# A decoder's output projection moved behind its attention, with query products among the heads

## The chip, the cores and the metric

One NeuronCore of a Trainium2 chip runs one program. The time is device microseconds of one execution. A core has TensorE (PE, matrix products, with PEld for its weight loads), VectorE (DVE), ScalarE (ACT) and GpSimd (POOL), each with an in-order queue of instructions; SP issues most transfers. TensorE writes to PSUM, in banks of 512 f32 columns by 128 partitions; everything else lives in SBUF, 128 partitions wide, or in device memory.

## What is computed

Two layers over `x`, 2 batches of 512 tokens by 1024, each a cross attention and a feed-forward part with a residual. The change is in the second layer's attention, all in f32 (abbreviated):

```python
x = x + _L1_xattn_ref(_layernorm(x), ctx_4096, ctx_4096, mask, wq, wk, wv, wo, 0)
x = x + _L1_ffn_ref(_layernorm(x), W_up, gate_w, expert_bias, lora_A, lora_B)

def _L1_xattn_ref(query, key, value, mask, wq, wk, wv, wo, curr_seq_pos):
    # 32 query heads, 8 key/value heads, 128 wide; 512 queries, 1024 keys
    q = rope(heads(query @ wq)); k = rope(repeat(heads(key @ wk))); v = repeat(heads(value @ wv))
    ...
```

then softmax of `q @ k.T / sqrt(128) + mask` over the keys, times `v`, the heads side by side (4096 wide), times `wo` (4096 x 1024).

## The kernel before

**Products in seven.** Every large product is cut in two by two blocks and computed with seven block products in place of eight (Strassen's scheme in Winograd's form): sums of the left blocks (`left_steps`), sums of the right blocks (`right_steps`), seven products, and sums of the results. `seven` (L258) makes a new result, `seven_onto` (L294) adds to rows that are there. `accumulate` (L343, the matmul is L345) issues one block product. An f32 matmul shows as two records in a trace.

**Queries.** `queries` (L664) makes the query heads, four at a time ("quads", eight of them); seven products of four 512-column matmuls give one head pair for both batches. Rope (L204 to L211) turns each result: two half copies on ACT, one product with the cosines on DVE (L207), a product with the sines and a sum (L210, L211) on DVE, or on POOL in the last quad. Seven quads run ahead of the attention, in a dense stretch; the last is spread over its first iterations.

**Attention.** `attention` (L851) is a software pipeline over 64 heads (batch 0's 32, then batch 1's). Iteration n issues three parts:
- scores of head n + 2 (L763, 8 matmuls of 512 columns); DVE adds the mask from PSUM (L777, four times);
- filler products on TensorE, and on DVE the maximum tree of head n + 2 over the keys (L785, L787, L789 of 1024 elements, L791 of 512; both inputs in SBUF), woven between the filler's own sums;
- transposes (L727) of head n's denominators, `turn_sum`, and later of head n + 2's maxima, `turn_maximum`, each followed by a reduction on DVE (L729) and a trip through device memory that spreads the row; the products with the values of head n (L826, 8 matmuls, in two halves); and for head n + 1 the exponential: DVE adds the negative maximum from PSUM (L809, 2048 elements, twice), ACT takes exp (L812, twice), POOL adds up the denominators (L815, L818, L819 of 1024 elements, L820 of 512).

POOL then normalises head n - 1 (L837). TensorE, DVE, ACT and POOL run in the written order here; transfers are ordered by the scheduler.

**The output projection** is the filler. A group of four heads (one key/value head) gives 512 of the 4096 columns; from iteration 5 on, `projection` (L839) adds a group's share to the rows of its batch: per 256 tokens by 1024, seven products of two 512-column matmuls, two of them for each row block. That is 14 block products a group, 3 or 4 (12 or 16 records) in each iteration, 28 matmuls a group and 448 in all. Its results are added on DVE (L312, L318) and on POOL (L300); the left sums of a group are four POOL instructions (L233 to L241). The sums of `wo` are made ahead, during the queries (`output_sums`, L692), and stored; `output_operand` (L709) loads them per group.

**Around it.** Rows of batch 0 are complete halfway through the attention, so its norm, statistics (L151, L152 in iterations 38 to 41) and transposes run among batch 1's heads, and its feed-forward part starts as the last heads end. SBUF is cut in slots: 14 of 8 KB, 17 of 4 KB, 10 of 2 KB per partition; PSUM in two double banks (`wide`, for scores and transposes) and four single ones (`b`).

## Time and profile before

| | us |
|---|---|
| median of 3 runs | 2437.01 (2436.92 to 2438.63) |
| profiled execution, span | 2432.8 |
| layer 1 and keys, values | 0 to about 640 |
| queries, dense | about 640 to 924 |
| attention: first to last score matmul | 924.5 to 2242.6 |
| last projections, feed-forward parts | to 2432.8 |

Between 1500 and 1600 us, well inside the attention, the engines were busy like this (stretch, its length, then busy time and instructions of PE, PEld, DVE, ACT and POOL, the granted clock, the DMA share and GB/s):

```profile
1500.00:1600.00 100.00, 100.00 (x259) 46.34 (x259) 86.65 (x78) 25.52 (x22) 73.26 (x37) 1.00 0.38 108
```

How to read what follows: a row of the timeline is start, length, engine, line, operation, result and inputs, partitions by elements, the number of merged instructions, and in brackets the idle time before it with what ended it. A matmul's end is modelled, and successive matmuls overlap by that tail, so the price of one is read from starts.

### The profile page before, as it was taken

To read this page: it belongs to the slowest core of one execution; us is meant where nothing else is said; L and a number is where in the kernel's file an instruction comes from. 1 tells how busy PE (TensorE), PEld (TensorE's weight loads), DVE (VectorE), ACT (ScalarE), POOL (GpSimd) and SP (SyncE) were. 2 spreads that over 40 slices of the span, in tenths; PEclk is the share of its full clock that TensorE was granted. 3 is DMA by queue.
4 is the path that set the end of the run, shared out by engine and by line. 5 is a ranking of instruction groups with operands and counts; after the bars stand their busy time and mean duration, and the time that the engine had idled before them with its cause. 6 is when DMAs were issued, how large, how long until landed. Compare 5 with 4: busy or idle time off the path is not lost.

```text
span 2432.8 us, 19529 instructions
## 1 busy us (share of the span) xinstructions
PE 2407.8 (99%) x6792; PEld 1195.1 (49%) x6792; DVE 1842.8 (76%) x1998; ACT 527.2 (22%) x623; POOL 1024.5 (42%) x543
## 2 busy tenths in 40 slices
PE   9999999999999999999999999999999999999999
PEld 4477458654444444444444444444444444444444
DVE  5849774345986556898888888888898988888753
ACT  1210221011222222322222222222223222222210
POOL 0000010210000002777676767667776767677531
PEclk9999999999999999999999999999999999999999
DMA  5437133013796221344223323442332243233501
GB/s 197 169 99 281 70 131 112 26 61 116 280 334 212 78 90 53 101 141 117 75 80 106 117 68 89 143 143 79 129 117 78 95 123 116 66 91 109 173 9 61
DMA packets 151506, 288.01 MB, mean 118 GB/s; under 512 B 32112, under 2 KB 49776, under 8 KB 149104
## 3 DMA queue, kind: packets, MB, share of 16 engines
q1 hardware_dynamic: 110880, 244.54, 30.6%
q10 hardware_dynamic: 40384, 41.70, 5.6%
q8 instruction: 54, 0.88, 0.1%
q0 software_dynamic: 144, 0.52, 0.1%
q14 instruction: 44, 0.36, 0.1%
HBM read 223.54 MB, written 63.18 MB: 118 GB/s over the span
## 4 chain that ended last, share of the span: by engine, by line
PE 55%; DVE 4%; issue 1%; POOL 0%; ACT 0%; POOLq 0%; DVEq 0%; ACTq 0%
PE b L345 20%; PE wide L763 16%; PE b L826 16%; PE wide L727 2%; DVE u L809 1%; DVE u L777 0%; DVE u L789 0%; DVE small L729 0%; DVE u L318 0%; DVE u L787 0%; PE b L967 0%; PE wide L192 0%; DVE u L791 0%; DVE u L785 0%; PE wide L1016 0%
## 5 line engine op out<-in xcount | busy, mean ns | idle before, releaser
L345 PE MATMUL b<-u,u 128*128 128x512 f32 (+1 forms) x3600 | 1384.5, 541 | 14.8 <-DVE u L283 4.2
L345 PEld LDWEIGHTS b<-u,u 128*128 128x128 f32 x3600 | 681.3, 191 | 684.0 <-issue 605.2
L826 PE MATMUL b<-u,u 128*128 128x512 f32 x1024 | 460.3, 592 | 0.0
L763 PE MATMUL wide<-u,u 128*128 128x512 f32 x1024 | 452.6, 593 | 2.6 <-DVE u L777 1.7
L815 POOL TENSOR_TENSOR u<-u 128x1024 f32<-128x1024 f32 x64 | 151.6, 2368 | 705.3 <-ACT u L812 696.8
L777 DVE TENSOR_TENSOR u<-wide,u 128x1024 f32<-128x1024 f32 x256 | 312.7, 1223 | 125.3 <-PE wide L763 125.1
L812 ACT ACTIVATE u<-u 128x2048 f32<-128x2048 f32 x128 | 244.7, 1911 | 665.1 <-DVE u L809 662.3
L763 PEld LDWEIGHTS wide<-u,u 128*128 128x128 f32 x1024 | 192.8, 190 | 250.9 <-issue 175.5
L809 DVE TENSOR_TENSOR u<-u,b 128x2048 f32<-128x2048 f32 x128 | 290.1, 2267 | 3.0 <-ACT b L805 3.0
L826 PEld LDWEIGHTS b<-u,u 128*128 128x128 f32 x1024 | 186.2, 192 | 184.6 <-issue 184.6
L300 POOL TENSOR_TENSOR u<-u,u 128x512 f32<-128x512 f32 x120 | 184.3, 1562 | 170.3 <-DVE u L312 134.6
L318 DVE TENSOR_TENSOR u<-u,b 128x512 f32<-128x512 f32 x200 | 135.6, 679 | 121.7 <-PE b L345 114.4
L818 POOL TENSOR_TENSOR u<-u,u 128x1024 f32<-128x1024 f32 x64 | 150.7, 2355 | 30.9 <-ACT u L812 30.7
L819 POOL TENSOR_TENSOR u<-u,u 128x1024 f32<-128x1024 f32 x64 | 150.8, 2356 | 5.0
L204 ACT ACTIVATE u<-u 64x512 f32<-64x512 f32 x72 | 45.2, 628 | 361.6 <-DVE u L283 162.5
L837 POOL TENSOR_TENSOR u<-u,u 128x512 f32<-128x512 f32 x64 | 115.0, 1797 | 18.4 <-DMA u<-row 18.4
L785 DVE TENSOR_TENSOR u<-u 128x1024 f32<-128x1024 f32 x64 | 113.0, 1765 | 0.0
L727 PEld LDWEIGHTS wide<-ident,u 128*128 128x128 f32 x512 | 79.9, 203 | 61.8 <-issue 55.7
L605 POOL TENSOR_TENSOR u<-u,u 128x1024 f32<-128x1024 f32 x8 | 20.2, 2528 | 213.0 <-DVE u L156 210.4
L787 DVE TENSOR_TENSOR u<-u,u 128x1024 f32<-128x1024 f32 x64 | 107.5, 1679 | 0.2
L820 POOL TENSOR_TENSOR u<-u 128x512 f32<-128x512 f32 x64 | 100.1, 1564 | 5.0
L1158 POOL DMA_DIRECT2D u<-in_b_dram x1 | 0.7, 717 | 229.1 <-PE b L345 229.1
(136 smaller groups left out, 1639.4 us busy)
## 6 DMA issues: line engine op xcount, KB each, us to landing
u<-row ACTq DMA_DIRECT2D x128, 256.0 KB, 3.5
u<-wo SPq DMA_DIRECT2D x64, 512.0 KB, 4.3
u<-in_wo_dram SPq DMA_DIRECT2D x48, 512.0 KB, 4.4
u<-in_wq_dram SPq DMA_DIRECT2D x32, 512.0 KB, 4.3
q<-u SPq DMA_DIRECT2D x64, 256.0 KB, 2.3
u<-in_wo_dram SPq DMA_DIRECT2D x16, 1024.0 KB, 8.0
wo<-u SPq DMA_DIRECT2D x32, 512.0 KB, 4.4
u<-q SPq DMA_DIRECT2D x64, 256.0 KB, 4.5
```

Source lines behind the costliest of these rows:

```text
L300: nc.gpsimd.tensor_tensor(c, c, what, ALU.add)
L318: nc.vector.tensor_tensor(c, c, acc, ALU.add)
L345: nc.tensor.matmul(acc, lhsT, rhs, start=start and k == 0, stop=k == len(pairs) - 1, skip_group_check=True,)
L727: nc.tensor.transpose(tr[:, t, :], src[:, t, :], ident)
L763: nc.tensor.matmul(sc[:, ts(n, HALF)], self.kT[:, ts(2 * j + n, P)], self.qT, start=True, stop=True,)
L777: nc.vector.tensor_tensor(self.e[j // 2][:, js, :], sc.rearrange("p (k q) -> p k q", k=2), mask[j], ALU.add)
L809: nc.vector.tensor_tensor(e, e, self.nmf.unsqueeze(1).to_broadcast([P, 4, S]), ALU.add)
L812: nc.scalar.activation(e, e, AF.Exp)
L815: nc.gpsimd.tensor_tensor(d, e[:, 0:2, :], e[:, 2:4, :], ALU.add)
L818: nc.gpsimd.tensor_tensor(d, d, e[:, 0:2, :], ALU.add)
L819: nc.gpsimd.tensor_tensor(d, d, e[:, 2:4, :], ALU.add)
L826: nc.tensor.matmul(self.acc, self.v[:, k, :], self.e[j][:, k % 4, :], start=(k == 0), stop=(k == NKT - 1),)
```

## The change

- The projection leaves the attention. Each head is normalised and stored, with the sums of the outer scheme made on POOL, as operands of seven products (`o_d[i]`, i = 1 to 7): `normalize` makes one difference of 256 elements, and for heads 16 to 31 three more sums with what `fetch_earlier` reloads of the head 16 before it.
- `two_level` computes each of the seven as seven again: 49 block products of 64, each 8 matmuls of 256 columns for either batch, 784 in all. Both batches share one weight operand. Its operand sums are DVE instructions (`tensor`), put off through `pending` in the attention.
- The first of the seven (`two_level(1, ...)`) starts in the attention, from iteration 56; the other six follow it, each with its loads made during the one before (`prefetch`).
- Query products become the filler. `query_unit` computes a unit (two heads for both batches) in seven steps of four 512-column matmuls; twelve units, 84 steps, go into iterations 2 to 55 by `count`; four begin before and end in iterations -2 to 1. Their weight sums are on DVE (four of 512 elements a unit: three at the first step, one at the second), their rope on DVE (L207's) and POOL (L210's and L211's). `chained` replaces `seven`, with fewer sums on DVE and more copies on ACT.
- The sums of `wo` (`output_sums`) move from DVE, ahead of the attention, to POOL in iterations 2 to 49: four of 512 elements in every three iterations.
- Heads alternate between the batches every four heads, so that a mask is fetched anew for each group of four (`fetch_mask`).
- The rows stay in device memory until the attention ends; the feed-forward part then takes token halves of both batches in place of batches.

```diff
...
+    def chained(product, emit):
+        at = {}
+        a = ps_b()
+        for i in (1, 2, 6, 5, 7, 3, 4):
+            if i in (2, 5):
+                c = ps_b()
+            acc = a if i in (1, 6, 7, 4) else c
+            product(i, acc, i in (1, 2, 5))
+            if i in (1, 6, 5):
+                at[i] = u2([P, HALF])
+                nc.scalar.copy(at[i], acc)
+            elif i == 4:
+                emit(1, 0, acc, True)
+            else:
+                held, place = {2: (1, (0, 0)), 7: (5, (1, 1)), 3: (6, (0, 1))}[i]
+                nc.vector.tensor_tensor(at[held], at[held], acc, ALU.add)
+                emit(*place, at[held])
...
+    def query_steps(q, m, eng, later):
+        def finish(i, j, src, in_psum):
+            dst = src
+            if in_psum:
+                dst = u2([P, HALF])
+                if later is not None:
+                    nc.scalar.copy(dst, src)
+                    src = dst
+            yield from rope_steps(dst, src, 0, ATT_SCALE, eng)
+            nc.sync.dma_start(q_d[j][4 * q + 2 * i + m], dst)
+        def emit(i, j, src, in_psum=False):
+            steps = finish(i, j, src, in_psum)
+            next(steps)
+            if later is None:
+                next(steps, None)
+            else:
+                later.append(steps)
+        return emit
...
+    def query_unit(q, m, h_ops, raw, s1, later, seven=chained):
+        w = dict(zip((1, 2, 7, 4), raw))
+        tensor = nc.vector.tensor_tensor
+        def product(i, acc, start):
+            accumulate(
+                acc, [(w[i][:, c, :], h_ops[i - 1][:, c, :]) for c in range(4)], start
+            )
+        for k, _ in enumerate(seven(product, query_steps(q, m, nc.gpsimd, later))):
+            if k == 0:
+                w[5] = s1()
+                tensor(w[5], w[7], w[4], ALU.add)
+                tensor(w[7], w[1], w[7], ALU.subtract)
+                w[6] = w[1]
+                tensor(w[6], w[5], w[1], ALU.subtract)
+            elif k == 1:
+                w[3] = w[2]
+                tensor(w[3], w[2], w[6], ALU.subtract)
+            yield k
...
+    def output_sums():
+        for c in range(NH // 2):
+            kq, c = divmod(c, 8)
+            t = u8([P, 2, 2, HALF])
+            for kh in range(2):
+                nc.sync.dma_start(
+                    t[:, kh], wo_v[:, 2 * kh + kq, c, :].rearrange("p (j n) -> p j n", j=2)
+            yield
+            b11, b12, b21, b22 = (t[:, kh, j] for kh in range(2) for j in range(2))
+            nc.gpsimd.tensor_tensor(b11, b12, b11, ALU.subtract)
+            nc.gpsimd.tensor_tensor(b12, b22, b12, ALU.subtract)
+            yield
+            nc.gpsimd.tensor_tensor(b22, b22, b11, ALU.subtract)
+            nc.gpsimd.tensor_tensor(b21, b21, b22, ALU.subtract)
+            for i, src in ((5, b11), (7, b12), (6, b22), (4, b21)):
+                nc.sync.dma_start(
+                    wo_t[i][:, kq, :, c, :], src.rearrange("p (q n) -> p q n", q=2)
+                )
+            yield
...
+            if self.n % GRP == GRP - 1 and self.n < B * NH - 1:
+                fetch_mask(1 - self.b, j)
...
+        def place(self, i):
+            return o_d[i][:, self.hd // 8 % 2, :, self.hd % 8, self.b, :]
+        def fetch_earlier(self):
+            self.earlier = u2([P, 2, 2, P])
+            for h, i in enumerate((0, 7)):
+                nc.sync.dma_start(self.earlier[:, h], self.place(i))
+            oT = self.oT
+            nc.gpsimd.tensor_tensor(oT, oT, self.den, ALU.mult)
+            halves = [oT[:, ts(h, QTR)].rearrange("p (t n) -> p t n", t=2) for h in range(2)]
+            more = u2([P, 2, 2, P])
+            diff = more[:, 0]
+            nc.gpsimd.tensor_tensor(diff, halves[1], halves[0], ALU.subtract)
+            if self.hd < NH // 2:
+                kept = {1: halves[0], 0: halves[1], 7: diff}
+            else:
+                hi, d = (self.earlier[:, h] for h in range(2))
+                nc.gpsimd.tensor_tensor(more[:, 1], d, halves[1], ALU.add)
+                nc.gpsimd.tensor_tensor(diff, d, diff, ALU.add)
+                nc.gpsimd.tensor_tensor(hi, hi, halves[1], ALU.add)
+                kept = {2: halves[0], 4: halves[1], 6: more[:, 1], 3: diff, 5: hi}
+            for i, t in kept.items():
+                nc.sync.dma_start(self.place(i), t)
+    total = B * NH
+    heads, kv, later, pending = {}, {}, [], []
...
+    def attention(fill, count, other, last):
+        for n in range(-2, total + 1):
+            fetch_values(n + 1)
+            if old and old.hd >= NH // 2:
+                old.fetch_earlier()
-            if n == GRP - 1 or n == NH:
-                fetch_rows(n // NH)
-            if GRP <= n <= total and n % GRP == 0:
-                oT = outs.pop(n // GRP - 1)
-                sums = u8([P, 3, 2, 256])
-                places = iter(range(3))
-                o_ops = left_sums(
-                    nc.gpsimd,
-                    oT[:, 0:2, 0:256],
-                    oT[:, 2:4, 0:256],
-                    oT[:, 0:2, 256:S],
-                    oT[:, 2:4, 256:S],
-                    lambda: sums[:, next(places)],
-                )
-                following = n // GRP - 1, o_ops
+            other(n)
-            k = (n - 1) % GRP
-            if n > GRP and k == 0:
-                gg, o_ops = following
-                stretches = projection(gg // NKV, o_ops, dict(w_ops))
-            for _ in range(3 + k % 2 if n > GRP else 0):
-                next(stretches, None)
-                next(tree, None)
-            if n > GRP and gg + 1 < B * NKV:
-                for i in {2: (1, 6, 2), 3: (7, 5, 4, 3)}.get(k, ()):
-                    w_ops[i] = output_operand((gg + 1) % NKV, i)
-            for i in range(extra.pop(n, 0)):
+            for i in range(count(n)):
-                next(extra["products"])
+                next(fill, None)
-            if n == GRP:
-                w_ops = {i: output_operand(0, i) for i in (1, 6, 2, 7, 5, 4, 3)}
-            if old:
+            if old and new:
+                if not new:
+                    old.turn_sum()
...
+            last(n)
+            yield
+    a_set, w_set = {}, {}
...
+    def first_sums(i):
+        a, w = a_set[i], w_set[i]
+        w["t1"] = [u4([P, 4, QTR]) for _ in range(2)]
+        for h in range(2):
+            yield tensor(w["t1"][h], w[0, 1][h], w[0, 0][h], ALU.subtract)
+            yield tensor(w[0, 1][h], w[1, 1][h], w[0, 1][h], ALU.subtract)
+        s1 = a["s1"] = u8([P, 8, B, P])
+        yield tensor(s1, a[0, 1], a[1, 1], ALU.add)
+        yield tensor(a[0, 1], a[0, 0], a[0, 1], ALU.subtract)
+    def two_level(i, block, fresh, op, put):
+        a, w = a_set[i], w_set[i]
+        banks = [ps_b(), ps_b()]
+        for k, (a_k, w_k, start, (x, y), first) in {
+            1: ((0, 0), (0, 0), True, (0, 0), True),
+            5: ("s1", "t1", True, (1, 1), True),
+            6: ((0, 0), (0, 0), False, (0, 1), True),
+            3: ("s1", (1, 1), False, (0, 1), False),
+            7: ((0, 1), (0, 1), False, (1, 1), False),
+            2: ((1, 0), (1, 0), True, (0, 0), False),
+            4: ((1, 1), "t1", False, (1, 0), True),
+        }.items():
+            acc = banks[k in (5, 3, 2)]
+            for b in range(B):
+                for c in range(8):
+                    nc.tensor.matmul(
+                        acc[:, ts(b, QTR)],
+                        a[a_k][:, c, b, :],
+                        w[w_k][c // 4][:, c % 4, :],
+                        start=start and b == 0 and c == 0,
+                        stop=c == 7,
+                        skip_group_check=True,
+                    )
+                if b == 0:
+                    yield
+            dst, src = block(x, y), acc.rearrange("p (b n) -> p b n", b=B)
+            if fresh and first:
+                nc.scalar.copy(dst, src)
+            else:
+                nc.vector.tensor_tensor(dst, dst, src, op)
+            if k == 1:
+                put(tensor(a[0, 0], a["s1"], a[0, 0], ALU.subtract))
+                for h in range(2):
+                    put(tensor(w[0, 0][h], w[1, 1][h], w["t1"][h], ALU.subtract))
+            elif k == 5:
+                put(tensor(a["s1"], a[1, 0], a[0, 0], ALU.subtract))
+            elif k == 7:
+                for h in range(2):
+                    put(tensor(w["t1"][h], w[1, 0][h], w[0, 0][h], ALU.subtract))
+            yield
...
+    def fill():
+        yield from chain(*early[:3])
+        raw = load_unit(2, 0)
+        yield from early[3]
+        for k in range(4, NH // 2):
+            for i in query_unit(*divmod(k, 2), h_ops, raw, lambda: u2([P, 4, P]), later):
+                if i == 4 and k + 1 < NH // 2:
+                    following = load_unit(*divmod(k + 1, 2))
+                yield
+            raw = following
+        r[0] = u8([P, 2, B, HALF])
+        yield from two_level(1, in_r, True, ALU.add, pending.append)
+    def count(n):
+        if n < 2:
+            return {-2: 6, -1: 6, 0: 4, 1: 4}[n]
+        if n > 55:
+            return (1, 1, 1, 1, 1, 1, 2, 2, 2)[n - 56]
+        upto = lambda k: 84 * min(k - 1, 54) // 54
+        return upto(n) - upto(n - 1)
...
+    def other(n):
+        if 2 <= n < 50:
+            next(out_sums)
+        for act in {
...
+            64: [lambda: load_a(2, 1, 1, late_4), lambda: load_a(2, 1, 0), lambda: load_rows_of(0)],
+        }.get(n, ()):
+            act()
+    def last(n):
+        if n == 53:
+            pending.extend(first_sums(1))
+        if n == 63:
+            pending.extend(first_sums(2))
+        room = 2
+        while pending and room > 0:
+            act = pending.pop(0)
+            room -= act.cost
+            act()
...
+    add_to(0, 0)
+    order = (2, 6, 5, 3, 7, 4)
+    for n, i in enumerate(order):
+        op = ALU.subtract if i == 3 else ALU.add
+        if i in (2, 3, 4):
+            s, j = {2: (0, 0), 3: (0, 1), 4: (1, 0)}[i]
+            block = lambda x_, y: x[s][x_][:, :, HALF * j + QTR * y : HALF * j + QTR * y + QTR]
+        else:
+            block = in_r
+        if i == 7:
+            r[0] = u8([P, 2, B, HALF])
+        if i == 6:
+            load_rows_of(1)
+        for k, _ in enumerate(two_level(i, block, i == 7, op, at_once)):
+            if n < 5:
+                prefetch(order[n + 1], k)
+            beside(i, k)
+        for where in {6: ((1, 0),), 5: ((0, 1), (1, 1)), 7: ((1, 0), (1, 1))}.get(i, ()):
+            add_to(*where, ALU.subtract if i == 7 else ALU.add)
...
```

## The prediction

> **What bounds the kernel now.** I read the page's busy shares first, then the instructions in order of time around the output projections, then the same two views for VectorE and GpSimd.
>
> ```profile
> PE 2407.8 (99%) x6792; PEld 1195.1 (49%) x6792; DVE 1842.8 (76%) x1998; ACT 527.2 (22%) x623; POOL 1024.5 (42%) x543
> ```
>
> TensorE is busy for 99% of the span, and its granted clock is 9 tenths or more in all 40 slices, so time is saved by issuing less to it and lost by making it wait. Next I need its price per record. Each f32 matmul leaves two records (a head's 8 score matmuls leave 16). The order of time gives starts; the last record's modelled tail (592 or 383 ns, its group's mean) is taken off:
>
> ```profile
> 516.72 7.07 PE L651 MATMUL b<-u,u 128*128 128x256 f32 x32
> ...
> 1026.70 7.03 PE L763 MATMUL wide<-u,u 128*128 128x512 f32 x16
> 1033.56 3.60 PE L345 MATMUL b<-u,u 128*128 128x512 f32 x8
> 1037.00 0.63 PE L727 MATMUL wide<-ident,u 128*128 128x128 f32 x4
> 1037.46 3.60 PE L826 MATMUL b<-u,u 128*128 128x512 f32 x8
> 1041.60 0.72 PE L727 MATMUL wide<-ident,u 128*128 128x128 f32 x4 [0.54 <-DVE u L791]
> 1042.16 3.60 PE L826 MATMUL b<-u,u 128*128 128x512 f32 x8
> 1045.59 7.42 PE L763 MATMUL wide<-u,u 128*128 128x512 f32 x16
> 1052.85 3.60 PE L345 MATMUL b<-u,u 128*128 128x512 f32 x8
> 1057.26 0.75 PE L727 MATMUL wide<-ident,u 128*128 128x128 f32 x4 [0.81 <-POOL u L820]
> ...
> 1062.32 0.72 PE L727 MATMUL wide<-ident,u 128*128 128x128 f32 x4 [0.87 <-DVE u L791]
> ...
> 1066.31 7.42 PE L763 MATMUL wide<-u,u 128*128 128x512 f32 x16
> ```
>
> A 512-column record costs (7.03 - 0.59) / 15 = 0.429 us, a 256-column one (7.07 - 0.38) / 31 = 0.216: exactly half. The rest of the fence shows the only two attention iterations of before that have just 8 filler records (n = 3 and 4) between scores and transposes. Undisturbed, one lasts 6.87 + 3.43 + 0.47 + 3.43 + 0.47 + 3.43 = 18.10 us. They lasted 18.89 and 20.72: TensorE waited 0.79 and 2.62, for VectorE's maximum tree (L791) and GpSimd's denominator sum (L820). With 12 or 16 filler records (19.82 and 21.54 each) it almost never waits. Why the tree is late:
>
> ```profile
> 1054.19 1.89 DVE L785 TENSOR_TENSOR u<-u 128x1024 f32<-128x1024 f32 x1
> 1056.12 2.17 DVE L787 TENSOR_TENSOR u<-u,u 128x1024 f32<-128x1024 f32 x1
> ...
> 1060.53 1.64 DVE L791 TENSOR_TENSOR u<-u 128x512 f32<-128x512 f32 x1
> ```
>
> ```profile
> 1055.08 2.12 POOL L820 TENSOR_TENSOR u<-u 128x512 f32<-128x512 f32 x1
> 1057.17 2.25 POOL L837 TENSOR_TENSOR u<-u,u 128x512 f32<-128x512 f32 x1
> ```
>
> They take turns. L820 starts at 1055.08 but ends 1.1 us after L785 does (1056.08); L787 starts at 1056.12 but ends 1.1 us after L820 (1057.20); L837 then ends 1.1 us after L787. Alone these forms take 1.2 to 1.3. VectorE's sums from PSUM (L777 1.22, L809 2.27) keep their times beside GpSimd.
>
> **The change, part by part.**
>
> 1. TensorE. Removed: 448 projection matmuls of 512 columns = 896 records x 0.429 = 384.4 us. Added: 7 x 7 x 16 = 784 of 256 columns = 1568 x 0.216 = 338.7. Query products, scores, attention and transposes keep their number. Net **-45.7**.
> The rule that speaks against narrower matmuls is the Trainium skill's, "TensorE: Matmul & The Clock Gate", Back-to-back issue gap: about 81 ns per matmul sustained at 128 columns but 131 at 512. Read linearly that makes 256 columns three quarters of 512, and the 1568 records 504 us, a loss of 120. The rows above say half.
>
> 2. The filler among the heads. Before, 12 or 16 records an iteration; now 84 query steps of 8 records in iterations 2 to 55. The pattern is 1,2,1,2,1,2,1,2,2, six times, and its 14 steps are exactly two query units. So 24 iterations have one step, 30 have two. From the last score to the maximum's transposes TensorE has 3.43 + 0.47 + 3.43 = 7.33 us of work with one step, 10.77 with two. VectorE needs, from the same point to the tree's end, 7.9 (1033.56 to 1041.45, L791's end) in one row above and 9.3 - 0.6 for one filler sum = 8.7 in the other (1052.85 to 1062.17); I take 8.3. A new unit adds, within that stretch, three 128x512 weight sums at its first step (SBUF alone, like L791: 0.69 alone, 1.16 in turns with GpSimd; 3.5), one such sum and a PSUM sum at its second (1.8), one PSUM sum (0.6) at its fifth and sixth. The nine iterations: first step alone 8.3 + 3.5 - 7.33 = 4.5; three others with one step 1.0 each; first and second step together 8.3 + 5.3 - 10.77 = 2.8; all else fits. 10.3 x 6 = **+62** (49 with 7.9, 73 with 8.7).
>
> 3. GpSimd's list. Gone: a projection's 10 sums per group of four heads (6 of L300, 4 of the left sums; 2.5 per head on average). New per iteration, at 1.22 us a 512 sum and half of that for 256: one 256 difference, three more for heads 16 to 31 (n from 33), 64 weight sums over iterations 2 to 49 (1.63), two rope operations for each of 48 outputs (2.17). That is 4.4 us, 6.2 in iterations 33 to 49, 4.6 to 55. The two rows give its price in a one-step iteration: with 2 extra operations (2.4 us) 0.25 us was lost beyond the tree's wait (0.79 - 0.54), with six (7.3) 1.75 (2.62 - 0.87). In between that is 0.86, 1.41 and 0.92, times some 14, 7.5 and 2.5 iterations = 25. For two-step ones the rows say 0 to 0.25 (21.54, and 21.79 to 21.81 where before had seven such sums): 3. **+28**, from 6 (all at 0.25) to 50 (all at 1.75).
>
> 4. Iterations 53 to 61. VectorE gets the first product's operand sums ahead of the next scores: 9.2 us from n = 53 on, some 6.9 more by 61, about eight pieces of 2.3. The nearest row is four iterations in which before puts L151 and L152 (1.5 us) there: the second half of the scores starts 0.3 to 0.8 late ("0.61 <-DVE u L777" is the longest wait). So some 0.9 is spare and a piece costs 1.4: 10. The six iterations from 56 have one step: 6 x (1.0 + 0.9) = 11. **+21**, from 6 (tree alone) to 35.
>
> 5. Of before's own waits 0.79 + 2.62 go, with 0.25 in each of 15 iterations and 2.0 at the statistics: **-9**.
>
> 6. At no price. The stage behind the heads loads 8 MB per product of 14 x 3.46 = 48.4 us, 173 GB/s; before moved 328 GB/s in 680 to 740 with TensorE at 60.00 of 60. Its operand sums (about 17 of SBUF work and 7 x 0.68 a product) hide under those 48.4, with GpSimd idle. The heads' stores (3 or 5 each), reloads, and masks (4 x 512 KB, now for every group) add 5 to 9 issues of 0.4 us per 20 us on SP, whose next due load, a query, has an iteration's slack. Last head to the second product: 3.4 for the denominator's rows, 3.7 on GpSimd, 2.3 store, 4.3 load, 2.3 sum = 16 against 20.7 of TensorE work; 0, at most 8 if the stores queue. SBUF slots (ten of 2 KB) now hold more tiles; no row prices a late one: 0, and the upper end allows for it.
>
> Sum: 2432.8 - 45.7 + 62 + 28 + 21 - 9 = 2489 of span. The runs' median, 2437.01, lies 4.2 above the span: **2493**. Its own range, with the low and the high ends added up: 2432.8 + 6 + 4.2 to 2432.8 + 111 + 4.2, so 2443 to 2548.
>
> **Rivals.** (a) *TensorE stays dense; faster.* If GpSimd's operations fall outside the tree, it ends 1.42 (the last mask sum's end behind the last score, 1531.37 less 1529.95) + 4.2 (1.33, 1.21, 1.21 and 0.69, the shortest of the four forms, each overlapping the next by 0.08) = 5.6 us after the scores, under 7.33, and only the first steps cost: about 2432.8 - 45.7 - 9 + 13 + 4.2 = 2395. For it: the three iterations from 962 to 1027 had rope operations on GpSimd (L210 and L211, eight in the first) and took 21.54 to 21.61. Against: these had two steps. It wins wherever all waits together stay under 54 us. Chance 0.24.
> (b) *GpSimd becomes the bound* in iterations 33 to 49. Its list alone: 8.4 (four denominator sums) + 1.25 + 6.2 = 15.9, and VectorE's SBUF operations hold it up for 3.9 (tree) + 1.0 = 4.9: 20.8 against a mean TensorE period of 20.0, before any wait for ScalarE's exponential. At 2 to 3 us more in 17 iterations: 2530 to 2545. Chance 0.10.
> The Trainium skill ("SBUF — State Buffer", SBUF: two separate sides) calls this port pair an exclusive lock held for a whole instruction, not a split of bandwidth; by it case (b)'s 20.8 is a floor, by a split it would be less. The turns above agree with the lock.
> (c) *Transfers bound the new stage.* 1 MB takes 7.6 to 8.0 us to land; eight in a row are 64 > 48.4, six times 15.6 = 94, with little waiting among the heads: about 2485. Against: the 328 GB/s. Or the narrow matmuls don't cost half. Together 0.06.
>
> **How the numbers follow.** The likeliest case has 0.60, of which 0.04 ends within 0.2% (about 5 us, what a measurement of this kernel can tell from no change). Faster 0.24, same 0.04, slower 0.56 + 0.10 + 0.06 = 0.72. The range runs from 2405 (leaving out the better half of (a)) to 2540 (leaving out the worse half of (b) and of the likeliest case's last stretch).
>
> **What would show it.** L763 records 1024 as before; 1568 new 256-column records at 0.216. One-step iterations of about 19 to 22 us in place of 18.1, with L727's idle put down to DVE's tree and POOL's sum, and L763's to the mask sums; the longest where a unit's first step stands alone. GpSimd above 80% busy among the heads against 71. The stage behind them dense. If the mean iteration is 20.0 us, part 2 is wrong; if TensorE idles behind the heads, part 6 is.

## The result, and the profile after

| | before | after |
|---|---|---|
| median of the runs | 2437.03 us (2436.92 to 2438.63, 4 runs) | **2517.22 us** (2516.75 to 2523.71, 4 runs) |
| profiled span | 2432.8 us | 2521.9 us |

The changed kernel is slower, by a ratio of 1.0334 (95% interval 1.032 to 1.0349). The forecast was 2493, in a range from 2405 to 2540. The profiled execution of after is the slowest of its four (2523.71; the others took 2516.75 to 2517.52), so the sums below, which come from it, stand some 6.5 us above the median.

Two lists carry the account below. Both come from the start times of TensorE's records. *Waits* are the gaps beyond the ordinary spacing of two records (where one draws the line moves a list by 1 to 2 us, and the difference of the two kernels by less). *Half-rate records* are records that start 0.85 us after the one before, where 0.43 is the rule. Before had 25.5 us of waits and 6.4 of half rate. After has 134.8 and 28.4, so 131.3 more in all. Less the 45.7 of TensorE work that went, that makes +85.6. The spans differ by 89.1.

The page of the changed kernel shows the engines, the new stage's matmuls (L1050), the scores (L814), the transposes (L771) and GpSimd's first denominator sum (L862):

```profile
PE 2402.1 (95%) x7456; PEld 1328.5 (53%) x7464; DVE 1871.4 (74%) x1786; ACT 550.1 (22%) x664; POOL 1240.3 (49%) x719
...
L814 PE MATMUL wide<-u,u 128*128 128x512 f32 x1024 | 471.0, 610 | 46.0 <-DVE u L822 40.0
...
L1050 PE MATMUL b<-u,u 128*128 128x256 f32 x1568 | 341.5, 379 | 1.4 <-DVE u L1017 1.4
...
L862 POOL TENSOR_TENSOR u<-u 128x1024 f32<-128x1024 f32 x64 | 151.5, 2367 | 171.2 <-ACT u L859 171.2
...
L771 PE MATMUL wide<-ident,u 128*128 128x128 f32 x512 | 87.9, 295 | 58.8 <-DVE u L838 37.7
```

The last column is the engine's idle time ahead of the group and what ended most of it. TensorE idles 46.0 us before scores (for VectorE's mask sums, L822, whose PSUM tile the scores need) and 58.8 before transposes (for the tree's last step, L838). The new stage itself waits for 1.4. Most of the rest ahead of the transposes is for GpSimd's denominators (L867): from 732 to 1926 us the view of waits has 36.1 us for L838 and 19.0 for L867. GpSimd idles 171.2 us before L862, waiting for ScalarE's exponential, so over the whole run its queue is not always full.

The view by stretches gives, for each 100 or 200 us, the busy time and records of PE, PEld, DVE, ACT and POOL, then the granted clock, DMA's share and GB/s:

```profile
932.00:1132.00 200.00, 188.72 (x482) 85.71 (x480) 179.76 (x142) 58.33 (x60) 159.67 (x85) 0.99 0.46 142
...
1532.00:1732.00 200.00, 188.63 (x469) 85.96 (x470) 178.18 (x140) 58.37 (x60) 179.71 (x108) 0.96 0.55 163
1732.00:1932.00 200.00, 179.03 (x448) 80.68 (x446) 165.86 (x134) 56.82 (x58) 151.75 (x95) 0.97 0.55 165
2100.00:2200.00 100.00, 98.62 (x458) 86.49 (x457) 57.94 (x47) 1.87 (x2) 5.03 (x7) 1.00 0.76 282
2200.00:2300.00 100.00, 100.00 (x465) 88.04 (x464) 55.78 (x51) 0.59 (x2) 0.00 (x0) 1.00 0.47 160
```

The stage behind the heads is dense: 465 records in 100 us, 0.215 us each. The loss lies among the heads. Over the six stretches of 200 us from 732 to 1932, three of them shown, VectorE is busy 83% to 92% and GpSimd 76% to 90%, and the granted clock is 0.96 to 1.00.

One iteration shows how it is lost: n = 11, where a query unit's first step stands alone. In the timeline (start, duration, engine, line, operation, what it waited for) it lasts from 925.62 to 949.44, 23.82 us where 18.10 is the undisturbed sum:

```profile
932.48 3.60 PE L371 MATMUL b<-u,u 128*128 128x512 f32 x8
...
933.83 2.13 DVE L832 TENSOR_TENSOR u<-u 128x1024 f32<-128x1024 f32 x1
934.95 2.13 POOL L867 TENSOR_TENSOR u<-u 128x512 f32<-128x512 f32 x1
935.99 2.17 DVE L834 TENSOR_TENSOR u<-u,u 128x1024 f32<-128x1024 f32 x1
...
937.04 2.25 POOL L895 TENSOR_TENSOR u<-u,u 128x512 f32<-128x512 f32 x1
937.13 0.75 PE L771 MATMUL wide<-ident,u 128*128 128x128 f32 x4 [1.05 <-POOL u L867]
...
938.08 1.75 DVE L735 TENSOR_TENSOR u<-u 128x512 f32<-128x512 f32 x1
939.36 1.05 POOL L899 TENSOR_TENSOR u<-u 128x256 f32<-128x256 f32 x1
939.87 1.10 DVE L736 TENSOR_TENSOR u<-u,u 128x512 f32<-128x512 f32 x1
941.07 0.69 DVE L738 TENSOR_TENSOR u<-u,u 128x512 f32<-128x512 f32 x1
941.67 1.22 DVE L836 TENSOR_TENSOR u<-u,u 128x1024 f32<-128x1024 f32 x1
942.93 0.69 DVE L838 TENSOR_TENSOR u<-u 128x512 f32<-128x512 f32 x1
...
943.76 0.89 PE L771 MATMUL wide<-ident,u 128*128 128x128 f32 x4 [2.45 <-DVE u L838]
...
944.45 5.15 PE L873 MATMUL b<-u,u 128*128 128x512 f32 x8
```

Three weight sums (L735, L736, L738) stand between the tree's second and third step. Up to 941 VectorE and GpSimd end alternately, each 0.5 to 1.1 us behind the other (935.96, 937.08, 938.16, 939.29, 939.83, 940.41, 940.97). From then on GpSimd is idle, and the last three VectorE sums take 0.69, 1.22 and 0.69; in turns the tree's 1024-column steps had taken 2.13 and 2.17. The tree ends 2.45 us late, and the eight records that follow take 5.15 in place of 3.60.

### The profile page after: what moved, and what is told of

It reads as the page before. It is cut to its first block, busy times and chain, and to the rows that moved or that the text cites. A ratio compares the mean times of both kernels' runs of the same rounds, so it can differ in the third digit from the quotient of the medians.

```text
span 2521.9 us, 21746 instructions
## 1 busy us (share of the span) xinstructions
PE 2402.1 (95%) x7456; PEld 1328.5 (53%) x7464; DVE 1871.4 (74%) x1786; ACT 550.1 (22%) x664; POOL 1240.3 (49%) x719
## 5 line engine op out<-in xcount | busy, mean ns | idle before, releaser
L371 PE MATMUL b<-u,u 128*128 128x512 f32 (+1 forms) x2704 | 990.4, 523 | 5.7 <-DVE u L285 3.8
L371 PEld LDWEIGHTS b<-u,u 128*128 128x128 f32 x2704 | 511.2, 190 | 452.1 <-issue 415.6
L814 PE MATMUL wide<-u,u 128*128 128x512 f32 x1024 | 471.0, 610 | 46.0 <-DVE u L822 40.0
L873 PE MATMUL b<-u,u 128*128 128x512 f32 x1024 | 474.9, 608 | 1.5 <-ACT u L882 1.5
L822 DVE TENSOR_TENSOR u<-wide,u 128x1024 f32<-128x1024 f32 x256 | 311.0, 1222 | 134.7 <-PE wide L814 117.8
L814 PEld LDWEIGHTS wide<-u,u 128*128 128x128 f32 x1024 | 196.2, 195 | 309.1 <-issue 199.1
L1050 PE MATMUL b<-u,u 128*128 128x256 f32 x1568 | 341.5, 379 | 1.4 <-DVE u L1017 1.4
L1050 PEld LDWEIGHTS b<-u,u 128*128 128x128 f32 x1568 | 297.3, 190 | 46.7 <-issue 4.9
L873 PEld LDWEIGHTS b<-u,u 128*128 128x128 f32 x1024 | 191.6, 197 | 194.6 <-issue 192.6
L326 POOL TENSOR_TENSOR u<-u,u 128x512 f32<-128x512 f32 x24 | 31.6, 1345 | 477.5 <-DVE u L338 460.7
L862 POOL TENSOR_TENSOR u<-u 128x1024 f32<-128x1024 f32 x64 | 151.5, 2367 | 171.2 <-ACT u L859 171.2
L1017 DVE TENSOR_TENSOR u<-u,u 128x1024 f32<-128x1024 f32 (+1 forms) x84 | 148.3, 1794 | 15.7 <-PE b L1050 13.6
L771 PEld LDWEIGHTS wide<-ident,u 128*128 128x128 f32 x512 | 77.2, 206 | 136.4 <-issue 92.4
L212 POOL TENSOR_TENSOR u<-u,sin_t 128x512 f32<-128x512 f32 x64 | 100.3, 1567 | 96.1 <-ACT u L207 88.4
L771 PE MATMUL wide<-ident,u 128*128 128x128 f32 x512 | 87.9, 295 | 58.8 <-DVE u L838 37.7
L834 DVE TENSOR_TENSOR u<-u,u 128x1024 f32<-128x1024 f32 x64 | 129.5, 2024 | 2.2
L895 POOL TENSOR_TENSOR u<-u,u 128x512 f32<-128x512 f32 x64 | 128.3, 2005 | 2.9 <-issue 2.9
```

The costliest lines, as they stand in the source:

```text
L371: nc.tensor.matmul(acc, lhsT, rhs, start=start and k == 0, stop=k == len(pairs) - 1, skip_group_check=True,)
L771: nc.tensor.transpose(tr[:, t, :], src[:, t, :], ident)
L814: nc.tensor.matmul(sc[:, ts(n, HALF)], self.kv[0][:, ts(2 * j + n, P)], self.qT, start=True, stop=True,)
L822: nc.vector.tensor_tensor(self.e[j // 2][:, js, :], sc.rearrange("p (k q) -> p k q", k=2), mask[j], ALU.add)
L862: nc.gpsimd.tensor_tensor(d, e[:, 0:2, :], e[:, 2:4, :], ALU.add)
L873: nc.tensor.matmul(self.acc, self.kv[1][:, k, :], self.e[j][:, k % 4, :], start=(k == 0), stop=(k == NKT - 1),)
```

## The experiments

The theory on trial: sums within SBUF, on VectorE and on GpSimd, make the tree and the mask sums late. The rivals: GpSimd's list alone sets the pace (G), or an iteration with one filler step is too short for its own chain, whoever sums (S).

**No weight sums.**

```diff
         for k, _ in enumerate(seven(product, query_steps(q, m, nc.gpsimd, later))):
+            if seven is chained:
+                if k == 0:
+                    w[5], w[6], w[3] = w[4], w[1], w[2]
+                yield k
+                continue
```

> Left out: the four sums per query unit of its weight tiles on VectorE (48 sums of 128x512, some 30 us of work alone); three of the seven products then use a tile that was not summed. All other work and its order stay. Theory (VectorE's maximum tree ends late in iterations with one filler step, because sums stand before it in VectorE's order and because it takes turns with GpSimd): the waits of 3.6 to 3.8 us where a unit's first step stands alone (n = 2, 11, 20, 29, 38) shrink to about 1, and those of 2.2 (n = 7, 16, 25, 34) to about 1; in all 40 us less than the changed kernel's 2517, so 2470 to 2482. Rival G (GpSimd's longer list alone sets the pace): nothing leaves GpSimd, so 2507 to 2517. Rival S (an iteration with one filler step is too short for the chain scores, mask, tree, maximum by itself, whoever else sums): 2505 to 2517.

2482.13 us (2480.09 to 2483.64), 35 less than after: at the theory's edge (0.1 above it), far from both rivals. The first-step iterations n = 2, 11, 20 and 29 now wait 1.5 to 1.7 us. Nothing left GpSimd here, so G alone cannot hold. But n = 38 and n = 47, where heads have four halves' sums on GpSimd, still wait some 5 us, mainly for GpSimd. The wait of n = 47, in after and in this run:

```profile
1726.85 1.13 PE L771 MATMUL wide<-ident,u 128*128 128x128 f32 x4 [4.44 <-POOL u L867]
...
1687.36 1.13 PE L776 MATMUL wide<-ident,u 128*128 128x128 f32 x4 [4.29 <-POOL u L872]
```

L872 is L867 of after, the last denominator sum. From 1694.5 to 1733.5 in after GpSimd was busy for 38.2 of 39.0 us. So in these two iterations of this run GpSimd's list is the bound, as G has it. From 732 to 1926 us the waits for the tree fell from 36.1 to 13.7 us, those for the denominators only from 19.0 to 16.8.

**No operand sums for the first product.**

```diff
+        if i == 1:
+            w["t1"], a["s1"] = w[0, 1], a[0, 1]
+            return
...
-            if k == 1:
+            if i == 1:
+                pass
+            elif k == 1:
```

> Left out: all operand sums of the new stage's first product (VectorE, between iterations 53 and 64; the products then read unsummed operands). Theory: the waits before scores in iterations 50 to 61 go and the tree is less late there: 22 us of waits and about 9 us of slower records behind long waits, so 2480 to 2492. Rival G: VectorE is not the bound in the tail: 2510 to 2517. Rival S: the one-step iterations of the tail go on waiting some 2 us each, 2500 to 2508.

2485.33 us (2484.86 to 2486.53), 32 less. Scores in n = 54 to 60 wait for nothing, and the one-step iterations there keep about 1 us each (19.3 us). The timeline of after shows what was taken away, in n = 54:

```profile
1870.01 6.03 DVE L1017 TENSOR_TENSOR u<-u,u 128x1024 f32<-128x1024 f32 x2
1875.96 2.34 DVE L822 TENSOR_TENSOR u<-wide,u 128x1024 f32<-128x1024 f32 x2
```

Two pieces of 1024 columns take 6.03 us, 3.0 each. The mask sums stand behind them, and the scores' second half waits 5.19 us.

**No output-weight sums.** The loads and stores stay.

```diff
-            nc.gpsimd.tensor_tensor(b11, b12, b11, ALU.subtract)
-            nc.gpsimd.tensor_tensor(b12, b22, b12, ALU.subtract)
             yield
-            nc.gpsimd.tensor_tensor(b22, b22, b11, ALU.subtract)
-            nc.gpsimd.tensor_tensor(b21, b21, b22, ALU.subtract)
```

> Left out: the 64 sums of the output projection's weights on GpSimd (128x512, about 1.22 us each alone, 78 us of its work); the loads and stores of these tiles stay, so the new stage gets unsummed weights. Theory: the tree waits less in turns with GpSimd only in the one-step iterations in which such sums ran: about 15 us less than 2517, so 2496 to 2508; the waits at a unit's first step stay at 3 us or more. Rival G: two sums of 1.2 us leave 32 iterations and GpSimd is the bound there: 30 to 45 us less, 2472 to 2487. Rival S: no change, 2512 to 2520.

2535.55 us (2535.31 to 2538.73): 18 *more*, with 78 us less work on GpSimd. No theory had this. The waits before scores grew from 47.1 to 71.8 us, in n = 9, 15, 24, 27 and 33 by 3.9 to 7.5 each, while those before transposes fell by some 16. In n = 9 (878 to 912 us) the view of waits (engine, line, what it waited for: total, times, longest) reads:

```profile
DVE u L818 <- DMA wo_t<-u: 4.3, 1, 4.3
```

A mask sum (L818 here) waited for a store of an output unit. The view names such a store in n = 15 and 33 too (5.8 and 4.7 us), in n = 27 the load of a row (7.2), and in n = 24 no transfer. Nothing but their load held the stores back now, and SP issued them at another place: four together, ahead of the values' load. The first stores of after, then this run's:

```profile
769.43 2.57 SPq L761 DMA_DIRECT2D wo_t<-u  x2
...
750.92 3.99 SPq L757 DMA_DIRECT2D wo_t<-u  x4
754.96 0.54 SPq L930 DMA_DIRECT2D u<-v  x1
```

**None of the new sums.** The three edits above together, and the sums of a head's halves go too.

```diff
-            nc.gpsimd.tensor_tensor(diff, halves[1], halves[0], ALU.subtract)
...
-                kept = {1: halves[0], 0: halves[1], 7: diff}
+                kept = {1: halves[0], 0: halves[1], 7: halves[1]}
...
```

> Left out: the sums of the three runs above together, and the differences and sums of a head's halves on GpSimd (one per head, four from head 16 on). The rotations on GpSimd stay, as do all matmuls, loads and stores. Theory: what remains of TensorE's waits among the heads is some 22 us of 121 and few slow records: 2400 to 2412, under the 2437 of the kernel before; so the price of the order itself is nearly nothing and the sums make all of the loss. Rival G (the rest of GpSimd's list, with the rotations, still bounds): 2440 to 2470. Rival S: a one-step iteration still takes 19 us or more in place of 18.1: 2450 to 2490.

2445.15 us (2439.83 to 2449.24): 33 above the theory's range, 5 under S's, inside G's. But the waits before transposes, where S and G would show, fell from 68.4 to 13.4 us; those before scores stayed at 47.7, again in single iterations (n = 3: 8.0, 27: 7.6, 33: 6.6). So the stores' place had to be held before this could be read.

**The same work cut to a few columns**, so that every store keeps its producer:

```diff
+            few = lambda t: t[:, 0:8]
-            nc.gpsimd.tensor_tensor(b11, b12, b11, ALU.subtract)
+            nc.gpsimd.tensor_tensor(few(b11), few(b12), few(b11), ALU.subtract)
...
```

> Left out: nearly all of the 64 output-weight sums on GpSimd; each is cut from 512 to 8 columns, so that the stores behind it keep their place in SP's queue (without the sums altogether, SP issued four stores together ahead of the values' load, and mask sums waited 4 to 8 us for that load). Theory: the waits for u<-v and at scores of 4 to 8 us in n = 9, 15, 24, 27, 33 are gone, and the tree's waits are shorter by some 15 us than the changed kernel's: 2496 to 2508. Rival G (GpSimd's list is the bound in 32 iterations): 2472 to 2490. Rival S: 2512 to 2520. If SP's queue was not what cost the 18 us: 2530 to 2540 again.

2504.54 us (2503.33 to 2506.75), 13 less than after and 31 less than without the sums altogether: inside the theory's range, 15 above G's. The cost in the run without them was in where the stores stood. Whether the mask sum waits for the unit's SBUF slot or for a place in a queue was not tried.

Then the sums of a head's halves in the same way (the tile that held them, `more`, goes too):

```diff
+            few = lambda t: t[:, :, 0:4]
-            nc.gpsimd.tensor_tensor(diff, halves[1], halves[0], ALU.subtract)
+            nc.gpsimd.tensor_tensor(few(h1), few(h1), few(halves[0]), ALU.subtract)
...
+                for t in (d, d, hi):
+                    nc.gpsimd.tensor_tensor(few(t), few(t), few(h1), ALU.add)
```

> Left out: as in the run above, and the differences and sums of a head's halves (one per head, four from head 16 on) are cut to 8 columns as well. Theory: no TensorE wait is for GpSimd's throughput, but less turn-taking lets the tree end earlier: 35 to 45 us less than 2517, 2470 to 2485, and the waits of a unit's first step alone stay above 2. Rival G: 2440 to 2465, with these waits gone. Rival S: 2510 or more.

2465.92 us (2465.47 to 2467.67), 51 less than after: 4 under the theory's range, 1 above G's. What tells them apart is the waits at first steps: 3.2 (n = 2) and 2.0 to 2.5 before transposes (n = 11 to 47) are still there, as the theory had it; G had them gone.

And with these cuts the first two edits of this section (no weight sums, no operand sums for the first product):

> Left out: GpSimd's sums as in the run above, VectorE's sums of the query weights and the operand sums of the new stage's first product. All matmuls, loads and stores and the rotations on GpSimd stay, and SP's order. Theory: TensorE's waits among the heads fall from 121 to 20 to 30 us, and slow records to under 5: 2400 to 2412, under the 2437 of the kernel before; the remaining 38 us of the run that left the same work out altogether were mask sums waiting for loads behind SP's stores. Rival S (a one-step iteration is too short by itself): 2435 to 2450, as in that run.

2402.30 us (2401.87 to 2403.32), a ratio to before of 0.9858 (0.9843 to 0.9873). The cuts were worth 13 (output weights), 39 (halves, on top of those), 35 and 32 us, together 118; all at once 115. Waits fell to 35.0 us and half rate to 7.8. That is 10.9 more than before had; with the 45.7 of TensorE work gone, the span should be 34.8 under before's, and it is 32.7 under (2400.1). This run's iteration n = 11 (915.39 to 933.60, 18.21 us), in the timeline:

```profile
922.25 3.60 PE L371 MATMUL b<-u,u 128*128 128x512 f32 x8
...
923.59 1.67 DVE L838 TENSOR_TENSOR u<-u 128x1024 f32<-128x1024 f32 x1
...
925.30 2.18 DVE L840 TENSOR_TENSOR u<-u,u 128x1024 f32<-128x1024 f32 x1
...
927.51 1.23 DVE L842 TENSOR_TENSOR u<-u,u 128x1024 f32<-128x1024 f32 x1
928.77 0.69 DVE L844 TENSOR_TENSOR u<-u 128x512 f32<-128x512 f32 x1
...
929.61 0.72 PE L777 MATMUL wide<-ident,u 128*128 128x128 f32 x4
930.16 3.60 PE L879 MATMUL b<-u,u 128*128 128x512 f32 x8
```

The same one filler step, and the tree ends at 929.46, before TensorE is free. S falls: a one-step iteration needs 18.1 to 19.4 us here, but for n = 53 (20.6). The stretches say the same (columns as before):

```profile
932.00:1132.00 200.00, 199.10 (x518) 92.06 (x517) 176.68 (x146) 64.85 (x67) 150.84 (x91) 1.00 0.52 159
...
1532.00:1732.00 200.00, 199.71 (x522) 92.39 (x521) 174.79 (x148) 65.99 (x68) 162.57 (x121) 1.00 0.66 197
```

TensorE is at 199 to 200 of 200 with VectorE at 87% to 88% busy. In these stretches of after it was at 89% to 90%: shares of busy time hardly tell the two cases apart.

The cut runs also need fewer tiles, so one could think that freed SBUF slots were the gain. Of the tree's four steps in after, from 732 to 1926 us, the last column shows otherwise:

```profile
L834 DVE TENSOR_TENSOR u<-u,u 128x1024 f32<-128x1024 f32 x54 | 113.7, 2106 | 1.9
L836 DVE TENSOR_TENSOR u<-u,u 128x1024 f32<-128x1024 f32 x54 | 100.0, 1851 | 0.8
L832 DVE TENSOR_TENSOR u<-u 128x1024 f32<-128x1024 f32 x54 | 93.8, 1738 | 5.6 <-PE b L371 5.6
...
L838 DVE TENSOR_TENSOR u<-u 128x512 f32<-128x512 f32 x54 | 57.6, 1066 | 1.9
```

VectorE idled 10.2 us ahead of them in 54 iterations, and for no transfer. The tree was late because VectorE was at work, its turns with GpSimd included.

**Two steps in each iteration.** 

```diff
-        upto = lambda k: 84 * min(k - 1, 54) // 54
-        return upto(n) - upto(n - 1)
+        return 2 if n < 44 else 0
```

> Nothing is left out. The 84 query steps come two an iteration in n = 2 to 43, and iterations 44 to 55 have none. Theory: with two steps the tree has 3.4 us more, so n = 2 to 43 lose 35 to 45 us in place of some 65; the ten to twelve empty ones wait some 4.7 us each and pay it back: 2525 to 2545, no gain. Rival S (one filler step is the fault, whoever sums): iterations with two steps wait for nothing in n = 2 to 43, and the empty ones wait 3.4 more than one-step ones: 2500 to 2515. Rival G (GpSimd's list paces an iteration): the period in n = 33 to 43 stays above 22.5, and the whole is 2500 to 2520, since GpSimd catches up nothing in the empty ones.

2525.75 us (2524.27 to 2526.71), as the theory had it. Iterations 2 to 43 lose 34.8 us (939.5 of time, 42 x 21.54 of work); n = 44 waits 8.1, and 45 to 53 wait 3.7 to 4.2 each. Even with two steps everywhere a unit's first step waits up to 3.4. An order of the filler moves the loss, it does not remove it.

**Later halves.** The differences and sums of halves go behind the rotations.

```diff
             rotate()
+            if n - 1 in heads:
+                heads.pop(n - 1).differences()
```

> Nothing is left out. The differences and sums of a head's halves move in GpSimd's order from before the rotations (beside the tree) to behind them (where GpSimd waits some 2 us a head for the exponential). Cutting them to 8 columns took 39 us off. Theory A (what counts is only what stands before or beside the tree): 2480 to 2500. Theory B (VectorE's sums within SBUF and GpSimd's operations share one resource, whose whole list is as long as TensorE's period: tree 4.2, denominators 8.3, normalising 1.25, differences 0.7 to 2.8, rotations 1.6 to 2.2, weights 1.6 and 0.9 a head, some 19 to 21 us against 20.0, so where a piece stands matters little): 2515 to 2540. Rival G (GpSimd's own list is the bound): 2510 to 2520, since the list is as long as before.

2521.75 us (2520.50 to 2524.79), where cutting them had been worth 39. Theory A falls: not only what stands beside the tree counts. B fits. G misses by 2, too little to tell it from B here; as the only cause it was out already with the weight sums.

**Plain first product.** Eight products of the operands as loaded, in place of seven with sums.

```diff
-        yield from two_level(1, in_r, True, ALU.add, pending.append)
+        yield from plain(1, in_r)
...
+        for x_, y in ((0, 1), (1, 1), (0, 0), (1, 0)):
+            acc = ps_b()
+            for kq in range(2):
...
+                            a[kq, x_][:, c, b, :],
+                            w[kq, y][c // 4][:, c % 4, :],
...
+            nc.scalar.copy(block(x_, y), acc.rearrange("p (b n) -> p b n", b=B))
```

> Nothing is left out. The new stage's first product is made of eight plain products in place of seven with operand sums: 32 more 256-column records (6.9 us of TensorE), 16 us fewer sums on VectorE among the last heads. Theory (sums in the tail cost 32 us there): 2517 - 32 + 7 = 2492, between 2484 and 2500. Rival S: the tail is bound by its order, 2515 to 2525.

2491.37 us (2485.62 to 2494.39), 26 less than after (ratio to before 1.0216, 1.0199 to 1.0233): 6.9 us more of TensorE took some 33 of waits and half-rate records away. The best version that computes the reference, and still slower than before.

**Six output-weight units earlier**, on top of it.

```diff
+        if n < 2:
+            for unit in early_units[max(0, 2 * n + 2):2 * n + 4]:
+                for _ in range(2):
+                    next(unit)
+            for unit in early_units[2 * n + 4:2 * n + 6]:
+                next(unit)
```

> Nothing is left out. The run above, and six of the sixteen output-weight units are summed in iterations -2 to 1, where GpSimd has little to do, so that the last are done by n = 31 in place of 49. Theory B: 4 to 8 us less than the run above, 2480 to 2494. If SP's earlier loads and stores hold up the masks or queries there: 2495 to 2515.

2509.70 us (2508.70 to 2511.97), 18 more than the run it stands on. From n = 33 to 53 it gained: 455.3 us against 463.2. But n = -2 to 1 took 147.2 us against 121.2. Of the waits in 660 to 760:

```profile
DVE u L829 <- DMA wo_t<-u: 27.2, 2, 15.7
...
PE b L371 <- DVE u L283: 12.1, 1, 12.1
```

Mask sums (L829) waited for the stores of output units, as above, and query products behind them.

**Another order in the tail.** Some of the first product's steps then read an operand before its sum is made.

```diff
-            return (1, 1, 1, 1, 1, 1, 2, 2, 2)[n - 56]
+            return (2, 2, 1, 1, 1, 1, 1, 2, 1)[n - 56]
```

> Nothing is left out. The first product's twelve steps among the last heads come as 2, 2, 1, 1, 1, 1, 1, 2, 1 in place of 1, 1, 1, 1, 1, 1, 2, 2, 2: the first two iterations, into which most operand sums fall, get more work on TensorE. Theory: only some 5 us of the tail's waits are covered: 2509 to 2518. Rival S (a one-step iteration is too short by itself): no change, 2515 to 2520, as many iterations have one step.

2528.66 us (2524.68 to 2529.68): a miss. Iterations 54 to 60 took 176.3 us against 175.0 with two steps (6.9 us) more in them, the 5 us expected. But then the last head's second half waited 6.9 us (1.6 in after) and the new stage 7.2 (1.5): the gain was given back at the end.

## Why the prediction was right, and where it was not

The direction, the place and the mechanism of the loss held; its size was 24 us low. Terms 2 to 5 come to +102, the lists above to +131; term 4 alone is 28 short. What it named as signs came: 1024 score records, 1568 new ones at 0.215, transposes idle for the tree and scores for mask sums, GpSimd at 83% from 732 to 1932 us (990.9 of 1200). First-step iterations took longer than the 19 to 22 us named, 22.1 to 28.7. Term by term:

1. *TensorE -45.7*: right. 0.215 us a 256-column record in the new stage, and the balance of the run with all sums cut to 2 us.
2. *Filler +62* and 3. *GpSimd's list +28*: together 90. Iterations 2 to 52 took 1115.2 us for 1019.4 of work (23 x 18.10 and 28 x 21.54), so 95.8 lost, some 14 of it at half rate, which no term had. The pattern of nine stands in the trace: a first step alone waits 3.6 to 3.8 us up to n = 29 (priced 4.5), first and second together 2.2 to 2.8 (2.8), most other one-step iterations 0.6 to 1.6 (1.0). In n = 38 and 47 the first step waits 6.1 and 4.6, in part or wholly for GpSimd's denominators. The split was off, and that the sum came so near is partly luck. Taking VectorE's weight sums away won 35, cutting GpSimd's sums 51. Part 2 charged all of a late tree to VectorE's sums, and part 3 priced GpSimd's by the loss beyond the tree. The runs show one account for both: VectorE's sums within SBUF and GpSimd's operations alternate, and what leaves either list brings the tree forward. The tree's own steps hardly got shorter by it: their means add up to 6.8 us in after and still to 6.2 with all sums cut, where an 8-column GpSimd sum beside them takes 1.05. What went is chiefly the work ahead of them and between them. The Trainium skill ("SBUF — State Buffer", SBUF: two separate sides) calls the port pair an exclusive lock for a whole instruction. The alternating ends and the near additive cuts agree with it.
4. *Iterations 53 to 61, +21*: mis-sized. They lost 44 up to n = 60 and 5 in n = 61; without the operand sums 32 of it went. The price per piece (2.3 us, 0.9 spare) came from before's short sums ahead of scores. (9.2 and 6.9 us make seven such pieces, not eight; the 10 in the sum is what seven cost.) In after a piece of 1024 columns took 3.0 us, two went ahead of one set of scores, and the wait of 5.19 brought 2.1 us of half-rate records.
5. *Before's own waits, -9*: a right order of size, too small to test. Not foreseen were 8.2 us of waits and half rate in n = -2 to 0, where before's own first iterations had 2.0. The run with all sums cut has them too (8.2), so the sums are not their cause; what is was not tried.
6. *At no price*: right for the stage behind (100.00 of 100) and for the last head (1.5 us). Wrong as a rule for SBUF slots or stores: in after they cost little, but three runs that moved them lost by it: 31 and 43 us against the same cuts with the stores in place, 18 against the run with the plain product.

The missing term is the half rate after waits: 28.4 us in after against 6.4. Rival (a), TensorE dense, would have needed the sums to be nearly free: with them cut the kernel takes 2402, near that rival's 2395, which still paid 13 for the weight sums. Rival (b) had the right resource, the sum of GpSimd's list and VectorE's SBUF sums, and was wrong to keep it to one stretch: n = 33 to 48 lost 2.3 us an iteration (357.6 for 320.6 of work), but n = 2 to 32 lost 1.6 (669.5 for 619.6). Within its stretch it came in n = 47, and in part in n = 38, where TensorE waits for GpSimd's denominators. Rival (c) did not come.

## What to carry to other kernels

A product saved by operand sums is paid for on the engines that sum. Where these share a resource with the work that TensorE waits for, add the lists of both engines per iteration and compare with TensorE's period, before asking where in the order a sum stands; a plain product can be cheaper (6.9 us of TensorE against 32). When an experiment leaves work out, keep a small piece of it as the producer of its stores: otherwise the transfers move, and the run measures that.

## What the runs showed of the hardware that was not expected

After a wait of TensorE the next two to five records often start 0.85 us apart, and then 0.43 again, and the granted clock of such stretches was 0.96 to 0.99 in the rows above, where the run with all sums cut has 1.00. In n = 11 above it followed a wait of 2.45 us. In n = 20 of the same kernel, with the same waits, it did not:

```profile
1140.12 0.72 PE L771 MATMUL wide<-ident,u 128*128 128x128 f32 x4 [2.46 <-DVE u L838]
1140.67 3.60 PE L873 MATMUL b<-u,u 128*128 128x512 f32 x8
```

What differs is where the wait falls. In the trace of after, each stretch at half clock lasts 3.41 us or twice that, and they begin whole numbers of 3.41 us apart (609.64, 749.59, 858.82 and 944.15 are 41, 32 and 25 such steps from one to the next). On that grid, the two iterations by the columns of the stretches (TensorE's busy time comes first, its granted clock third from the end):

```profile
940.74:944.15 3.41, 0.96 (x5) 0.42 (x4) 3.27 (x5) 0.00 (x0) 0.00 (x0) 1.00 0.83 233
944.15:947.56 3.41, 3.41 (x7) 1.64 (x7) 3.38 (x5) 0.92 (x1) 0.00 (x0) 0.50 0.61 231
...
1135.30:1138.71 3.41, 2.36 (x6) 0.76 (x4) 3.27 (x4) 0.00 (x0) 1.39 (x2) 1.00 0.60 130
1138.71:1142.12 3.41, 2.00 (x8) 1.32 (x9) 3.34 (x5) 0.00 (x0) 0.00 (x0) 1.00 0.91 338
1142.12:1145.53 3.41, 3.41 (x10) 1.50 (x9) 3.41 (x3) 1.91 (x1) 0.56 (x1) 1.00 1.04 394
```

In n = 11 the whole wait lies in one window, 2.45 us idle of 3.41, and the next window has clock 0.50. In n = 20 it is split, 1.05 in one window and 1.41 in the next, and the clock stays at 1.00. Counted over all windows of after from 612 us on that were themselves at full clock, those with a half-clock window behind them had 1.96 us of idle or more, the others 1.91 or less. In before none had more than 0.97 between 612 and 2400 us, and none was followed by half clock. So whether a wait of 2 to 3 us costs half-rate records depends on where it falls on this grid. The Trainium skill ("TensorE: Matmul & The Clock Gate", What's actually happening) puts the fall to half rate at an idle window of about 3.4 us. The length agrees with the 3.41 here, but the window need not be idle throughout: 1.96 us was enough.
